# Splitting the last superblock of a graph network's edge loop and moving the work around it

## The chip, the core and the metric

The kernel runs on one core of a Trainium2 chip. The core has five engines that run on their own and meet at semaphores: TensorE (PE in the profile, with PEld for its weight loads), VectorE (DVE), ScalarE (ACT), GpSimd (POOL) and SyncE (SP). Data moves through 16 DMA engines that all queues share. The metric is the device time of one execution in microseconds; the median of the runs counts.

## The reference

A graph of 6250 nodes and 100,000 edges goes through two layers of typed attention and a final layer norm. Node types are 0 to 15, edge types 0 to 31; there are 8 heads of 16. Cut to what matters:

```python
def gt_layer(x, ntype, etype, src, dst, Wk, Wq, Wv, Wa, Watt, Wmsg, pri, skip, g, b):
    k, q, v = (typed_linear(x, ntype, W).reshape(n, H, HS) for W in (Wk, Wq, Wv))
    kT = jnp.einsum('nhd,htdo->nhto', k, Watt)      # one row per node and edge type
    vT = jnp.einsum('nhd,htdo->nhto', v, Wmsg)
    kw = kT[src, :, etype]
    m = vT[src, :, etype]
    a = jnp.einsum('ehd,ehd->eh', kw, q[dst]) * pri[:, etype].T / SQRT_D
    att = edge_softmax(a, dst, n)
    hag = jax.ops.segment_sum((m * att[:, :, None]).reshape(-1, H * HS), dst, num_segments=n)
    h = jax.nn.silu(typed_linear(hag, ntype, Wa))
    alpha = jax.nn.sigmoid(skip[ntype])[:, None]
    h = h * alpha + x * (1.0 - alpha)
    mu = jnp.mean(h, axis=-1, keepdims=True)
    var = jnp.mean((h - mu) ** 2, axis=-1, keepdims=True)
    return (h - mu) * jax.lax.rsqrt(var + 1e-05) * g + b

for l in range(2):
    h = gt_layer(h, ...)
x = _layernorm(x + h @ ff_w + ff_b)
```

## The kernel before

**Tables.** Each layer has a table in DRAM with one row of 256 numbers (`kT` and `vT`, 1 KiB) for every node and edge type. The first layer's table is written during preparation, from the input `x`. The second layer's is written while the first layer runs, from its results. No gather of layer 1 may start before every row of its table is written; a dependency from all the table scatters to the first gather of layer 1 sees to that (lines 969 to 976).

**Nodes in blocks.** Preparation sorts the nodes by class of type and by degree and puts them into 50 blocks of 128. Block `b` has `KB[b]` slots, as many as the largest number of edges into one of its nodes; all blocks together have 867. Class `c` of types (four types each) owns ten blocks with 25, 22, 20, 19, 18, 17, 16, 16, 15 and 14 slots; the other ten blocks hold nodes of mixed types. Blocks are worked on in superblocks of up to four, listed in `sbs` (lines 783 to 792), 15 of them. The last four are: superblock 11, blocks 46 to 49 (mixed, 38 slots); 12, blocks 30 to 33 (86 slots); 13, blocks 34 to 36 (18, 17 and 16 slots); 14, blocks 37 to 39 (16, 15 and 14 slots).

**The edge loop** (`edges`, line 833, once for each layer). For each slot of a block GpSimd issues one indirect DMA that fetches 128 table rows (128 KiB) into `kv` (line 966). Four slots make a chunk; there are 12 chunk buffers. VectorE multiplies a chunk by the queries (line 978) and adds up over each head (line 982). `finished` (line 875) then makes a block's softmax and weighted sums, as a generator whose steps are taken between the chunks of the next block. The last block of a superblock hands its sums to `nodes`.

**Nodes** (line 1056) is a long chain for a whole superblock: normalizing (`hag`, line 1014), transposes, the typed linear `wa` with one mask for each type, tanh, mixing with the old row (`hs`, line 1083), the layer norm with some twelve tiny VectorE instructions, transposes again. In layer 0 the linears for the next layer's keys, values and queries follow (line 1136), and then `pieces_of` (line 1177) makes table rows: for a block, two halves of 16 edge types each, built in `st` (16 KiB in each partition) by 16 small matmuls and PSUM copies on ScalarE (lines 262 to 269), and sent off by GpSimd as an indirect scatter of 2 MiB (line 1183). A block has two such scatters, and `st` has three buffers. The last superblock (`final`, line 1059) shares the copies between ScalarE and VectorE. In layer 1 a linear `ffw`, the addition of `x` and a second layer norm follow, and each block's result goes out by one indirect scatter on GpSimd (line 1216). If the superblock is not `final`, the result is first held in `results` and leaves after a number of further chunks (`leave`, line 862).

**The order.** The program is straight-line code. GpSimd executes in the order in which the program text issues, gathers and scatters in one queue; on the other engines a scheduler at compile time may move an instruction that it holds to be ready ahead of others. The order itself is made by `tick` (line 846): after each of the three parts of a chunk it takes steps of the first generator in `work` (queries and nodes) and of the first in `pieces` (table rows). How many depends on the rate given to `spread`: so many steps over so many gathers. For `nodes` the rate is 34, 46 or 50 steps over `pace(s + 1)`, the slots of the next superblock without half of its first block. For table rows it is 8 steps for each block and 4 more over the slots of superblock `s + 2`, or over 0.6 of them for the last four superblocks. What is left in both lists when the gathers end is issued then (lines 996 to 1003).

**Buffers that count here.** The pool `npl` of the node chain gives most of its tiles one buffer (`hs`, `th`, `mv`, `bn`, `v`), four to the masks `xm`; the node chain has two PSUM buffers (`nb`), the table rows three (`tb`).

Of the kernel before, what the change touches and what calls it, by code (L numbers as in the profile page):

```python
# [27 lines left out]
NC = 4  # L28
# [68 lines left out]
def kernel(  # L97
# [31 lines left out]
    TC = TY // NC  # L129
# [90 lines left out]
    def superblocks(n):  # L220
        k = -(-n // SB)
        for c in range(k):
            yield n * c // k, n * (c + 1) // k - n * c // k
# [216 lines left out]
    with tc.tile_pool(name="tp", bufs=2) as tp, \  # L440
# [302 lines left out]
        sbs = list(superblocks(NT))  # L743
# [26 lines left out]
    def arm(fast):  # L770
# [3 lines left out]
        outs_put, results = [], []  # L774
# [8 lines left out]
        sbs = []  # L783
        if fast:

            mixed = [(NC * CB + i0, k, range(TY)) for i0, k in superblocks(1 + RB)]
            for c in range(NC):
                for i0, k in reversed(list(superblocks(CB))):
                    sbs.append((c * CB + CB - i0 - k, k, range(c * TC, (c + 1) * TC)))
                sbs += mixed[c * len(mixed) // (NC - 1):(c + 1) * len(mixed) // (NC - 1)]  # L790
        else:
            sbs = [(i0, k, range(TY)) for i0, k in superblocks(NB)]
# [40 lines left out]
        def edges(l):  # L833
# [4 lines left out]
            got, work, pieces = [], [], []  # L838
# [3 lines left out]
            def spread(work, gen, steps, slots):  # L842

                work.append([gen, steps / slots, 0.0])
# [12 lines left out]
            def rush(of, gen):  # L857
                while any(w[0] is gen for w in of):
                    for _ in of.pop(0)[0]:
                        pass  # L860
# [8 lines left out]
            def slots(s):  # L869
                return sum(KB[b] for b in range(sbs[s][0], sbs[s][0] + sbs[s][1]))  # L870
# [4 lines left out]
            def finished(s, i, chunks, kvt, a, sums, den):  # L875


                i0, k, _ = sbs[s]
                K = KB[i0 + i]
                av = a[:, :K, :]  # L880
                nc.vector.tensor_tensor(
                    av, av, neg[:, KO[i0 + i]:KO[i0 + i] + K].unsqueeze(2)
                    .to_broadcast([P, K, H]), op=ALU.add)
                yield
                m = ep.tile([P, H], F32, name="m")
                nc.vector.tensor_reduce(m, av.rearrange("p k h -> p h k"), axis=AX.X, op=ALU.max)
                yield
                nc.vector.tensor_tensor(av, av, m.unsqueeze(1).to_broadcast([P, K, H]),  # L888
                                        op=ALU.subtract)
                nc.scalar.activation(av, av, AF.Exp)  # L890
                yield
                yield
                nc.vector.tensor_reduce(den[:, i, :], av.rearrange("p k h -> p h k"),
                                        axis=AX.X, op=ALU.add)

                acc = ep.tile([P, CH, D], F32, name="acc", bufs=1)
                for j in range(len(chunks) + 1):
                    if j < len(chunks):
                        j0, j1 = chunks[j]
                        v = kvt[j][:, :j1 - j0, D:]  # L900
                        nc.vector.tensor_tensor(  # L901
                            (v if j else acc).rearrange("p k (h d) -> p k h d", h=H),
                            v.rearrange("p k (h d) -> p k h d", h=H),
                            av[:, j0:j1, :].unsqueeze(3).to_broadcast([P, j1 - j0, H, HS]),
                            op=ALU.mult)
                    if j > 1:
                        j0, j1 = chunks[j - 1]
                        nc.vector.tensor_tensor(acc[:, :j1 - j0], kvt[j - 1][:, :j1 - j0, D:],  # L908
                                                acc[:, :j1 - j0], op=ALU.add)
                    yield  # L910
                nc.vector.tensor_reduce(sums[:, i, :], acc.rearrange("p k c -> p c k"),
                                        axis=AX.X, op=ALU.add)
                if i == k - 1:
                    spread(work, nodes(l, *sbs[s], sums, den, got[s][1], lambda gen: table(s, gen)),
                           50 if l else 34 + (12 if len(sbs[s][2]) > TC else 0), pace(s + 1))

            def pace(s):
                s = min(s, len(sbs) - 1)
                return slots(s) - 0.5 * KB[sbs[s][0]]
# [3 lines left out]
            def table(s, gen):  # L923


                if gen is None:
                    if s - 2 in tables:
                        rush(pieces, tables[s - 2])
                else:
                    tables[s] = gen  # L930
                    spread(pieces, gen, 8 * sbs[s][1] + 4, (1.0 if s + 4 < len(sbs) else 0.6) * slots(min(s + 2, len(sbs) - 1)))

            before = iter(())
            q = query(0, 0)
            for s, (i0, k, types) in enumerate(sbs):
# [6 lines left out]
                for i in range(k):  # L942
# [17 lines left out]
                    for j0, j1 in chunks:  # L960
                        c = j1 - j0
# [30 lines left out]
                    if not then:  # L992
                        step(end=True)
                    before = finished(s, i, chunks, kvt, a, sums, den)
                    q = then[0] if then else None
            for _ in before:
# [3 lines left out]
            while work or pieces:  # L1000
                for of in (work, pieces, pieces, pieces):
                    if of and next(of[0][0], of) is of:
                        of.pop(0)

        def normalized(acc, den, i0, k):
            rd = ep.tile([P, SB, H], F32, name="rd")
            nc.vector.reciprocal(rd[:, :k], den[:, :k])
            yield
            nc.vector.tensor_tensor(
                rd[:, :k], rd[:, :k],  # L1010
                nonempty[:, i0:i0 + k].unsqueeze(2).to_broadcast([P, k, H]), op=ALU.mult)
            yield
            hag = ep.tile([P, SB, D], F32, name="hag", bufs=1)
            nc.vector.tensor_tensor(  # L1014
                hag[:, :k].rearrange("p i (h d) -> p (i h) d", h=H),
                acc[:, :k].rearrange("p i (h d) -> p (i h) d", h=H),
                rd[:, :k].rearrange("p i h -> p (i h)").unsqueeze(2).to_broadcast([P, k * H, HS]),
                op=ALU.mult)
            return hag
# [194 lines left out]
        def put_out(o, i0, i):  # L1214
            b = i0 + i
            put = nc.gpsimd.indirect_dma_start(  # L1216
                out=out, out_offset=bass.IndirectOffsetOnAxis(ap=node[:, b:b + 1], axis=0),
                in_=o[:, i, :], in_offset=None, bounds_check=N - 1, oob_is_err=False)

            if fast:  # L1220
                for other in outs_put:
                    tc.declare_no_dep(put.ins, other.ins, reason="rows of other nodes")
                outs_put.append(put)
# [69 lines left out]
        for l in range(L):  # L1293
            if l == 0:
                for i, w in enumerate((Wk, Wv, Wq)):
                    load_typed(wkqv[:, i], w[1])
                load_edge_weights(1)
                if not fast:
                    scale_edge_weights()
            else:  # L1300
                load_typed(wa, Wa[1])
            if fast:
                edges(l)
            else:
                edges_any(l)

    full = nc.values_load(over[0:1, 0:1], min_val=0, max_val=1)
    with tc.If(full < 1) as cmp:  # L1308
        with ExitStack() as ctx2:
            ctx2.enter_context(tc.manual_schedule(engines={mybir.EngineType.Pool}))  # L1310
            arm(True)
    with cmp.Else():
        with ExitStack() as ctx2:
            arm(False)
# [46 lines left out]
```

## Time and profile before

| | us |
|---|---|
| median of 3 runs (lowest, highest) | 3544.61 (3541.61, 3552.11) |
| the profiled execution | 3932.2 |
| its span, first to last instruction | 3930.4 |
| first gather of layer 0 starts | 843.5 |
| last gather of layer 0 starts | 2405.5 |
| first gather of layer 1 starts | 2497.5 |
| last gather of layer 1 starts | 3879.9 |
| last output scatter starts | 3922.3 |

The profiled execution is 388 us longer than the median, so its times are compared among themselves. Over the whole span the engines are busy for these shares, and in 40 equal slices for these tenths (PEclk is the clock granted to TensorE, the last two rows are the DMA engines):

```profile
PE 1974.2 (50%) x7142; PEld 887.1 (23%) x7142; DVE 2232.3 (57%) x4900; ACT 833.8 (21%) x1366; POOL 2104.1 (54%) x2032
## 2 busy tenths in 40 slices
PE   4999998950556367655766867202111122021212
PEld 2444553320222123222222323001010111010111
DVE  4787684424736456555745744346446465564746
ACT  1444434430123113421343144100000000000000
POOL 0000005637566566667556763476576676766764
PEclk9999999965667677677767777655555555555555
DMA  5676648793265346755566578533232233323321
GB/s 137 274 305 278 267 194 323 308 319 96 86 240 203 130 154 218 286 200 199 196 247 213 170 280 312 196 100 89 83 95 88 83 98 92 104 85 88 101 85 49
```

A slice is 98 us. Slices 0 to 8 are the preparation, 9 to 24 layer 0, and from 25 on layer 1, where ScalarE and TensorE have little to do. No engine is busy throughout: 54% of POOL is an average over a preparation without gathers and two loops with them.

### The profile page before, as it was taken

What the parts mean: (1) busy time and instruction counts of PE and PEld (TensorE: products, weight loads), DVE (VectorE), ACT (ScalarE), POOL (GpSimd) and SP (SyncE); (2) the same over time, 40 slices, a digit from 0 to 9 for tenths busy, and PEclk for the clock granted to TensorE, in tenths of its full rate; (3) what the DMA queues carried; (4) which work ended last, traced back from release to release, by engine and by line L of the source; (5) the groups of instructions that cost most, each with busy time, mean ns of one, the idle gap of its engine ahead of it and who ended that gap; (6) DMA issues with size and microseconds to landing.
All of it is one profiled execution on the core that took longest, in us unless ns stands there. A gap on an engine that the chain in (4) does not pass through costs nothing. (4 is left out here: it accounts for less than half of the span.)

```text
span 3930.4 us, 25592 instructions
## 1 busy us (share of the span) xinstructions
PE 1974.2 (50%) x7142; PEld 887.1 (23%) x7142; DVE 2232.3 (57%) x4900; ACT 833.8 (21%) x1366; POOL 2104.1 (54%) x2032
## 2 busy tenths in 40 slices
PE   4999998950556367655766867202111122021212
PEld 2444553320222123222222323001010111010111
DVE  4787684424736456555745744346446465564746
ACT  1444434430123113421343144100000000000000
POOL 0000005637566566667556763476576676766764
PEclk9999999965667677677767777655555555555555
DMA  5676648793265346755566578533232233323321
GB/s 137 274 305 278 267 194 323 308 319 96 86 240 203 130 154 218 286 200 199 196 247 213 170 280 312 196 100 89 83 95 88 83 98 92 104 85 88 101 85 49
DMA packets 201147, 694.54 MB, mean 177 GB/s; under 512 B 61382, under 2 KB 111896, under 8 KB 175946
## 3 DMA queue, kind: packets, MB, share of 16 engines
q0 software_dynamic: 105424, 448.83, 34.2%
q1 hardware_dynamic: 72924, 234.11, 15.3%
q10 hardware_dynamic: 22642, 9.82, 1.1%
q8 instruction: 60, 0.98, 0.1%
q14 instruction: 97, 0.79, 0.1%
HBM read 268.12 MB, written 429.48 MB: 177 GB/s over the span
## 5 line engine op out<-in xcount | busy, mean ns | idle before, releaser
L966 POOL DMA_INDIRECT kv<-tab,ell x1734 | 1806.1, 1042 | 786.2 <-issue 501.0
L269 ACT COPY st<-tb 128x512 f32<-128x512 f32 (+1 forms) x976 | 683.1, 764 | 743.1 <-PE tb L262 458.4
L978 DVE TENSOR_TENSOR kv<-kv,q 128x512 f32<-128x512 f32 (+3 forms) x468 | 301.7, 647 | 469.2 <-DMA kv<-tab,ell 426.2
L732 PE MATMUL l<-xm,wkqv 128*128 128x512 f32 (+1 forms) x832 | 385.8, 599 | 54.8 <-DVE xm L232 54.8
L247 PE MATMUL nb<-ident,hag 128*128 128x128 f32 x100 | 25.4, 390 | 763.0 <-DVE hag L1014 350.1
L232 DVE SCALAR_TENSOR_TENSOR xm<-ntb,nb 128x384 f32<-128x384 bf16 (+1 forms) x336 | 186.7, 593 | 245.2 <-remote 158.4
L982 DVE TENSOR_REDUCE a<-kv 128x32 f32<-128x512 f32 (+3 forms) x468 | 297.2, 639 | 29.4 <-remote 6.5
L262 PE MATMUL tb<-bdv,kvT 32*128 32x512 f32 x800 | 276.5, 817 | 43.5 <-ACT st L269 24.8
L241 PE MATMUL nb<-xm,wa 128*128 128x384 f32 (+1 forms) x384 | 219.1, 731 | 151.2 <-DVE xm L232 91.0
L262 PE MATMUL tb<-bdk,kvT 32*128 32x512 f32 x800 | 256.4, 814 | 57.8 <-ACT st L269 35.5
L890 ACT ACTIVATE a<-a 128x128 f32<-128x128 f32 (+12 forms) x100 | 31.9, 319 | 1143.3 <-DVE a L888 487.1
L1183 POOL DMA_INDIRECT tab<-st,row x100 | 110.2, 1102 | 306.7 <-ACT st L269 265.7
L908 DVE TENSOR_TENSOR acc<-kv,acc 128x512 f32<-128x512 f32 (+3 forms) x368 | 233.2, 634 | 57.7 <-remote 47.6
L901 DVE TENSOR_TENSOR kv<-kv,a 128x512 f32<-128x512 f32 (+3 forms) x368 | 231.0, 636 | 0.0
L267 DVE COPY st<-tb 128x512 f32<-128x512 f32 (+1 forms) x208 | 149.2, 718 | 121.9 <-PE tb L262 88.4
L732 PEld LDWEIGHTS l<-xm,wkqv 128*128 128x128 f32 x832 | 149.0, 193 | 286.7 <-issue 199.1
L232 DVE SCALAR_TENSOR_TENSOR xm<-ntb,hT 128x512 f32<-128x512 int32 (+1 forms) x208 | 133.8, 658 | 139.7 <-PE l L732 102.1
L247 PE MATMUL nb<-ident,hs 128*128 128x128 f32 x100 | 32.1, 456 | 353.8 <-DVE hs L1094 274.9
L241 PE MATMUL nb<-xm,wq 128*128 128x384 f32 (+1 forms) x192 | 104.3, 704 | 179.4 <-DVE xm L232 159.1
L247 PEld LDWEIGHTS nb<-ident,hag 128*128 128x128 f32 x100 | 15.2, 193 | 781.7 <-issue 568.2
L720 POOL DMA_DIRECT2D ntb<-in_node_type_dram x13 | 7.3, 558 | 341.9 <-DVE xm L232 341.9
L262 PE MATMUL tb<-bdv,yT 32*128 32x512 f32 x784 | 169.7, 658 | 4.7 <-ACT st L269 3.5
(234 smaller groups left out, 2678.0 us busy)
## 6 DMA issues: line engine op xcount, KB each, us to landing
tab<-st SPq DMA_DIRECT2D x98, 2048.0 KB
kv<-tab,ell POOLq DMA_INDIRECT x1734
hr<-xrd SPq DMA_DIRECT2D x20, 192.0 KB
xrd<-xr POOLq DMA_DIRECT2D x11, 256.0 KB
hr<-in_x_dram POOLq DMA_DIRECT2D x10, 256.0 KB
ntb<-in_node_type_dram POOLq DMA_DIRECT2D x10, 256.0 KB
hr<-xrd SPq DMA_DIRECT2D x10, 256.0 KB
ntb<-typed SPq DMA_DIRECT2D x20, 96.0 KB
```

The costliest lines, as they stand in the source:

```text
L232: nc.vector.scalar_tensor_tensor(xm[:, :n], ntb[:, :n], float(t), hT[:, :n], op0=ALU.is_equal, op1=ALU.mult)
L241: nc.tensor.matmul(ps[:, :n], w[:, t, :], xm[:, :n], start=(t == types[0]), stop=(t == types[-1]))
L262: nc.tensor.matmul(pt[:, b], yT[s, i * P:(i + 1) * P], bd[s, tt, :], start=True, stop=True)
L267: nc.vector.tensor_copy(to, pt)
L269: nc.scalar.copy(to, pt)
L732: nc.tensor.matmul(ps[i][:, :n], wkqv[:, i, t, :], xm[:, :n], start=(t == 0), stop=(t == TY - 1))
L901: nc.vector.tensor_tensor((v if j else acc).rearrange("p k (h d) -> p k h d", h=H), v.rearrange("p k (h d) -> p k h d", h=H), av[:, j0:j1, ...
L908: nc.vector.tensor_tensor(acc[:, :j1 - j0], kvt[j - 1][:, :j1 - j0, D:], acc[:, :j1 - j0], op=ALU.add)
L966: get = nc.gpsimd.indirect_dma_start(out=kv[:, j - j0, :], out_offset=None, in_=tabs[l][:], in_offset=bass.IndirectOffsetOnAxis(ap=ell[:, ...
L978: nc.vector.tensor_tensor(kk, kk, q.unsqueeze(1).to_broadcast([P, c, D]), op=ALU.mult)
L982: nc.vector.tensor_reduce(a[:, j0:j1, :], kk.rearrange("p k (h d) -> p k h d", h=H), axis=AX.X, op=ALU.add)
L1183: put = nc.gpsimd.indirect_dma_start(out=tabs[1].rearrange("(n t) c -> n (t c)", t=16), out_offset=bass.IndirectOffsetOnAxis(ap=row2[:, tg ...
```

## The change

In the list of superblocks the last one, blocks 37 to 39, is cut into blocks 37 and 38 and block 39 alone; there are 16 superblocks then, and only the last counts as `final`. The order of the blocks and of the gathers stays. Node steps of the last three superblocks are spread over 0.6 of `pace`. Table pieces of the last five (the same superblocks as the last four before, since there is one more) are spread over 0.4 of the slots in place of 0.6. For superblocks 12 and 13 these slots are fewer, too, since superblock `s + 2` is now smaller: 31 slots in place of 45 for 12, 14 in place of 45 for 13. After the loop that empties `work` and `pieces`, results that are still held are put out.

```diff
@@ -787,6 +787,10 @@
             for c in range(NC):
                 for i0, k in reversed(list(superblocks(CB))):
                     sbs.append((c * CB + CB - i0 - k, k, range(c * TC, (c + 1) * TC)))
+                if c == NC - 1:
+
+                    i0, k, types = sbs.pop()
+                    sbs += [(i0, k - 1, types), (i0 + k - 1, 1, types)]
                 sbs += mixed[c * len(mixed) // (NC - 1):(c + 1) * len(mixed) // (NC - 1)]
@@ -912,7 +916,8 @@
                     spread(work, nodes(l, *sbs[s], sums, den, got[s][1], lambda gen: table(s, gen)),
-                           50 if l else 34 + (12 if len(sbs[s][2]) > TC else 0), pace(s + 1))
+                           50 if l else 34 + (12 if len(sbs[s][2]) > TC else 0),
+                           (0.6 if s + 3 >= len(sbs) else 1.0) * pace(s + 1))
@@ -928,7 +933,7 @@
                     tables[s] = gen
-                    spread(pieces, gen, 8 * sbs[s][1] + 4, (1.0 if s + 4 < len(sbs) else 0.6) * slots(min(s + 2, len(sbs) - 1)))
+                    spread(pieces, gen, 8 * sbs[s][1] + 4, (1.0 if s + 5 < len(sbs) else 0.4) * slots(min(s + 2, len(sbs) - 1)))
@@ -1001,6 +1006,8 @@
                 for of in (work, pieces, pieces, pieces):
                     if of and next(of[0][0], of) is of:
                         of.pop(0)
+            while results:
+                put_out(*results.pop(0)[1])
```

## The prediction

> **What bounds the kernel now.** I read the busy times by stage first, then GpSimd's (POOL's) instructions in order of time at the two places where the gathers end, then VectorE (DVE), ScalarE (ACT) and TensorE (PE) there. The chain that ended last is of no use: it holds only the last output scatters. By stage (us, busy time and count of each engine, granted clock, DMA share, GB/s):
>
> ```profile
> 1205.00:2406.00 1201.00, 769.00 (x2230) 315.29 (x2227) 698.32 (x1547) 355.87 (x466) 762.79 (x728) 0.73 0.60 213
> 2406.00:2497.00 91.00, 65.83 (x237) 26.24 (x237) 32.93 (x68) 38.93 (x49) 12.50 (x13) 0.74 0.75 303
> 2497.00:3881.00 1384.00, 242.63 (x607) 138.41 (x607) 778.71 (x1988) 44.77 (x123) 950.64 (x911) 0.53 0.32 92
> 3881.00:3931.00 50.00, 13.88 (x35) 8.22 (x35) 24.58 (x95) 1.26 (x3) 8.45 (x6) 0.53 0.04 12
> ```
>
> Layer 1 (third row) is a stream of POOL issues: 911 of them, 950.6 us busy, and 0.30 us of sequencing ahead of most, so 1224 of 1384 us. The change adds none there. What it can move is the second row (91 us between the layers, 12 table scatters, no gather) and the fourth (50 us after the last gather). POOL in order of time at the first (start us, us, engine, line, operation):
>
> ```profile
> 2384.53 1.01 POOL L1183 DMA_INDIRECT tab<-st,row  x1 [0.30 <-issue]
> 2390.87 1.01 POOL L1183 DMA_INDIRECT tab<-st,row  x1 [0.30 <-issue]
> ...
> 2405.54 0.95 POOL L966 DMA_INDIRECT kv<-tab,ell  x1 [0.31 <-issue]
> 2416.52 1.01 POOL L1183 DMA_INDIRECT tab<-st,row  x1 [10.03 <-ACT st L269]
> ...
> 2464.65 0.97 POOL L1183 DMA_INDIRECT tab<-st,row  x1 [15.49 <-ACT st L269]
> 2467.25 0.97 POOL L1183 DMA_INDIRECT tab<-st,row  x1 [1.62 <-DVE st L267]
> 2470.57 0.97 POOL L1183 DMA_INDIRECT tab<-st,row  x1 [2.35 <-DVE st L267]
> 2475.98 0.97 POOL L1183 DMA_INDIRECT tab<-st,row  x1 [4.43 <-DVE st L267]
> 2481.14 0.98 POOL L1183 DMA_INDIRECT tab<-st,row  x1 [4.19 <-DVE st L267]
> 2486.91 0.97 POOL L1183 DMA_INDIRECT tab<-st,row  x1 [4.79 <-issue]
> 2497.51 0.99 POOL L966 DMA_INDIRECT kv<-tab,ell  x1 [9.63 <-issue]
> ```
>
> The reader is to see three things: a scatter per four gathers (every 6.3 us) while gathers last; 92.0 us from the last gather of layer 0 to the first of layer 1; and scatters some 5 us apart once pieces are plentiful. That 5 us is the transfer: one scatter is 2 MiB, and between 2470 and 2490 us the DMA share is 1.0 at 419 to 429 GB/s, so 4.9 us each. The stretch from 2286 to 2497 us moves 28 scatters (59 MB) and 66 gathers (8.7 MB), 158 us at that rate; about 50 us of DMA idleness is all that reordering could win between the layers.
>
> VectorE and POOL at the end of the kernel:
>
> ```profile
> 3893.60 0.56 DVE L1014 TENSOR_TENSOR hag<-sums,rd 128x384 f32<-128x384 f32 x1
> ...
> 3919.68 0.98 POOL L1216 DMA_INDIRECT out_dram<-o,node  x1 [25.50 <-DVE o L1169]
> 3920.97 0.98 POOL L1216 DMA_INDIRECT out_dram<-o,node  x1 [0.30 <-POOLq L1308]
> 3922.26 0.98 POOL L1216 DMA_INDIRECT out_dram<-o,node  x1 [0.30 <-issue]
> ```
>
> The last gather starts at 3879.9; 13.7 us later the last sums are normalized, and 26.1 us after that the last superblock's results leave.
>
> **What the Trainium skill says.** "DMA: Bandwidth & Descriptors", Specifications, gives a fabric ceiling of 435 GB/s; the 429 GB/s of the final scatters agrees. Its section on the anatomy of a SWDGE DMA adds about 2 us of fixed cost to each; in a row of scatters the trace shows 5.0 to 5.8 us, so the fixed part overlaps, and I use the trace. "PSUM — Partial Sum Buffer", Engine vs sequencer instructions, calls the ScalarE, VectorE and GpSimd queues strict FIFO; the trace agrees: at 2416.52 POOL stood 10.03 us for one piece, with nothing behind it overtaking. This is what the slower rival rests on.
>
> **The change part by part.** I number superblocks 0 to 15 as after; 13 is the same in both, 14 was blocks 37 to 39 (16, 15 and 14 slots) and becomes 37 and 38, with 39 alone as 15. Walking the pace rule of the loop through both programs gives where scatters stand among the 867 gathers; the walk of the old program lies on the trace scatter for scatter. Before: superblock 11's eight between gathers 805 and 830, 12's eight between 834 and 857, 13's and 14's six each after gather 867. After: 11's between 801 and 818, 12's between 826 and 834, 13's six between 850 and 853, and only 14's four and 15's two after 867. The node steps of 13 still begin at 838 but end at 850, not 867.
>
> Loop of layer 0. Sixteen scatters now stand ahead of gather 835, too dense to hide: 16 x 5.0 us plus 33 gathers x 0.3 us (128 KiB at 429 GB/s) = 90 us. From 2284 (the first scatter was issued at 2286.2 after a stand of 8.0 us; being four gathers earlier helps it little) this is 2374, where gather 834 was at 2343.0. Sixteen gathers free of scatters at 1.25 us: 2394 (before 2378.2). Then 13's six scatters, two intervals at ACT's copying rate (four copies of 0.93 us) and three at 5.0, some 24 us with what lies between: 2418. Fourteen gathers at 1.25 us: the last at 2436. It was 2405.5, so **+30 us**.
>
> Between the layers. Before, 92.0 us. After: finishing block 39 took 19.0 us to 2424.5, of which 9.0 were a stand for ACT, busy with 13's copies, that are gone now: 10. The chain of the last superblock, from `hag` at 2424.5 to its first scatter at 2464.65, took 40.1; 7.7 of these were a stand of VectorE for PE behind 13's matmuls, also gone; one block instead of three shortens matmuls (9.5 us for the three linears, 4.2 for the first), masks (1.95) and evacuations, and I take 10 of the some 20 us that scale: 22.4. Superblock 14's chain runs beside it and they share single buffers (`hs`, `th`), two PSUM buffers and four masks: 0 to 10, I take 6. A second scatter 3, and its landing and the wait of the first gather 10.6 as before. Sum 52, so **-40 us**. Superblock 14 itself is not late: its sums are there when the last gathers are issued, a two-block chain is some 26 us, and four scatters follow by then plus 15. Between the layers with the loop: -10.
>
> Layer 1 and the end. Gathers, scatters and output scatters keep their counts, so the POOL stream stays. Node steps of 13 end at gather 846 instead of 865, which frees VectorE at the end of some 4 us (its statistics and normalizing lay between 3879.9 and 3888.3). Superblock 14's chain can start at block 38's sums, 3885.3 in the trace, two or three us sooner so freed; a two-block chain is 26.1 less about 6, plus 4 for block 39's finishing beside it: 3906. Block 39's chain cannot overlap all of it: `mv` has one buffer, held until the last use of 14's means at its output step, so 15 runs from its `mv` on after that: 15.1 us in the trace (3904.6 to 3919.7) less six of nine matmuls (4 us) and about 1 of narrower steps: 10. First output scatter 3916, and the two held results of 14 leave behind it at 1.29 us each; the last starts at 3918.7, not 3922.3: **-3.5 us**. That the held results leave once the work is emptied is needed, since 14 is no longer the final one; it costs no issue, as three stand at the end in both. The extra superblock adds one query load of layer 1 and one small query stage of layer 0 (some 4 transposes and matmuls and 3 evacuations), beside gathers, near nothing; if not covered, 3 us.
>
> Sum: -10 - 3.5 = -13 against the profiled execution's 3932.2 us (span 3930.4). The unprofiled median is 388 us lower; I cannot see from this trace where those go, though issues of POOL are many enough. My terms are transfer times and dependency chains, so I carry -13 over whole: 3544.6 - 13 = **3532 us**.
>
> **The rivals.**
> - *Slower: POOL stands for superblock 13's first piece.* Place: its scatters at gather 850, ahead of the last 17 gathers in POOL's queue. The chain of 13 took from `hag` at 2335.0 to 2416.5, 81.5 us, while mixed with 12's pieces on PE and ACT. Gather 822 would be at about 2330, sums 14 us later as before (2319.3 to 2333.4), so the chain starts at 2345. I assume it is done by 2394, since it is spread over 12 gathers instead of 29 and a free chain is 40.1 - 7.7 = 32 us. If it takes 81.5 again, POOL stands 33 us: -13 + 33 = +20, 3565. Up to 13 us the gain stays; from 24 us on it is slower by more than 0.3%. For it: PE and ACT issue 12's pieces ahead. Against: more of these are done by then.
> - *Full gain.* Denser pieces of 11 start at 2276, where their first copy was (8 us sooner), and the two last chains don't hinder each other (6): -27, 3518. For it: DMA has the room. Against: the stands on ACT that the trace shows already.
> - *Nothing: what leaves the boundary is paid in the loop.* Gathers share DMA with dense scatters, and each lands behind up to three of them (15 us); if 11 of these are exposed at block 38 or 39, the sum is -2: 3543. For it: loop and boundary differ by +30 and -40, each of that size by estimate.
>
> **How the numbers follow.** Forecast 0.45, full gain 0.15, nothing 0.15, slower 0.25. A measurement tells about 0.3% from no change, 10.6 us. Of the forecast 0.40 is beyond that, so faster 0.55, same 0.20, slower 0.25. The forecast's own range is 3522 to 3540. The whole range goes down past the full gain with sums ready earlier, 3512, and up to most of the slower rival, 3560.
>
> **What would show it.** In the profile after: 22 scatters before layer 0's last gather and six after; that gather some 30 us later than 2405.5; the gap to layer 1 near 52 us; POOL's idle time before 13's first scatter under 13 us; layer 1's gather stream at 1384 us; and the last output scatter 38 to 40 us after the last gather. A long stand of POOL at gather 850, a gap still over 75 us, or a layer 1 that moves by over 10 us would make the prediction wrong.

## The result and the profile after

| | before | after |
|---|---|---|
| median, us (runs; lowest to highest) | 3541.61 (7; 3533.27 to 3554.62) | 3576.00 (7; 3567.71 to 3595.64) |
| ratio after to before, 95% interval | 1 | 1.0091 [1.0065, 1.0118] |

The change makes the kernel slower by 0.9%, some 32 us. The forecast was 3532 us, faster; 3576 lies above its range.

One thing has to be known before two profiles are laid side by side. Chips differ. On one of them the same kernel takes 3920 us without a profiler, too (first experiment), and its profile there agrees with the one that the prediction reads (spans 3900.5 and 3930.4, layer 1 1384.2 and 1382.4 us); I take that one to come from such a chip. The profile of after (span 3573.4) came from one at the speed of the medians. So after is compared here with a later profile of before at that speed (span 3555.3, a run of 3557.1 us, experiment `e9_before_third`). I number gathers of layer 0 from 1 to 867 and cut the time at gathers 801, 835, 850, 854, 867, the first gather of layer 1 and its last gather. Busy time by stretch, first before, then after (start and end, length, busy time and count on PE, PEld, DVE, ACT and POOL, granted clock, DMA share, GB/s):

```profile
2087.00:2153.00 66.00, 49.39 (x183) 19.63 (x183) 35.05 (x78) 38.38 (x45) 44.64 (x44) 0.77 0.81 295
2153.00:2182.00 29.00, 21.61 (x73) 8.75 (x71) 18.92 (x53) 14.81 (x19) 20.01 (x20) 0.65 0.99 375
2182.00:2191.00 9.00, 6.88 (x20) 2.51 (x20) 1.17 (x2) 6.70 (x7) 5.75 (x7) 0.61 1.01 404
2191.00:2210.00 19.00, 17.15 (x48) 8.02 (x46) 11.49 (x23) 4.96 (x9) 13.50 (x14) 0.73 0.95 372
2210.00:2295.00 85.00, 61.91 (x222) 24.20 (x220) 33.61 (x69) 36.19 (x46) 13.26 (x15) 0.75 0.80 323
2295.00:3506.00 1211.00, 232.09 (x607) 137.79 (x607) 770.24 (x1986) 44.98 (x123) 922.43 (x911) 0.54 0.36 105
```
```profile
2070.00:2162.00 92.00, 74.75 (x269) 29.66 (x265) 35.38 (x81) 57.24 (x65) 51.08 (x50) 0.74 0.89 344
2162.00:2183.00 21.00, 11.08 (x21) 5.64 (x22) 13.53 (x45) 1.18 (x3) 14.33 (x15) 0.58 0.83 300
2183.00:2226.00 43.00, 32.23 (x118) 11.58 (x116) 12.86 (x25) 24.78 (x30) 10.02 (x11) 0.82 0.69 273
2226.00:2244.00 18.00, 5.12 (x12) 3.10 (x12) 10.68 (x35) 0.79 (x2) 13.74 (x15) 0.50 0.63 219
2244.00:2308.00 64.00, 38.29 (x160) 20.04 (x160) 20.57 (x59) 22.99 (x35) 7.06 (x8) 0.74 0.60 233
2308.00:3522.00 1214.00, 234.08 (x607) 138.34 (x607) 770.86 (x1989) 44.50 (x122) 925.35 (x911) 0.53 0.36 104
```

Read three columns. Length: the first stretch grew from 66 to 92 us, the third (four gathers) from 9 to 43; the gap between the layers shrank from 85 to 64; layer 1 stayed. ACT's busy time: before, copies for table rows run through all of the loop's end (14.8, 6.7 and 5.0 us in the second to fourth row); after, ACT has 1.2 us of work in 21 and 0.8 in 18, and 24.8 between them. DMA share: 0.99, 1.01 and 0.95 before while the last 32 gathers were issued, 0.83, 0.69 and 0.63 after. The old order kept the DMA engines full with evenly spread scatters. The new one sends them in bursts; between these ACT has next to nothing to do, PE is busy for a half and a quarter of the time, and DMA is not filled.

At the place where 13's scatters stand now, POOL after, in order of time:

```profile
2183.39 0.95 POOL L971 DMA_INDIRECT kv<-tab,ell  x1 [0.30 <-issue]
2196.52 1.02 POOL L1190 DMA_INDIRECT tab<-st,row  x1 [12.18 <-ACT st L269]
...
2207.71 0.97 POOL L1190 DMA_INDIRECT tab<-st,row  x1 [2.88 <-ACT st L269]
...
2224.91 1.30 POOL L1190 DMA_INDIRECT tab<-st,row  x1 [11.06 <-ACT st L269]
2226.51 1.35 POOL L971 DMA_INDIRECT kv<-tab,ell  x1 [0.30 <-issue]
...
2243.80 0.94 POOL L971 DMA_INDIRECT kv<-tab,ell  x1 [0.30 <-issue]
2268.40 1.01 POOL L1190 DMA_INDIRECT tab<-st,row  x1 [23.65 <-ACT st L269]
...
2294.71 0.97 POOL L1190 DMA_INDIRECT tab<-st,row  x1 [13.59 <-ACT st L269]
2297.23 0.97 POOL L1190 DMA_INDIRECT tab<-st,row  x1 [1.54 <-issue]
2307.60 0.99 POOL L971 DMA_INDIRECT kv<-tab,ell  x1 [9.40 <-DMA tab<-st,row]
```

Twice POOL stands for a table piece while 17 and 14 gathers are queued behind it: 12.18 us for 13's first, 11.06 us for its sixth. After the last gather it stands 23.65 us for 14's first piece and 13.59 us for 15's. Why 13's first piece is so late is seen earlier, on PE, ACT and VectorE (in this order):

```profile
2155.89 3.70 PE L262 MATMUL tb<-bdv,kvT 32*128 32x512 f32 x8
2159.52 0.90 PE L247 MATMUL nb<-ident,hag 128*128 128x128 f32 x3
```
```profile
2145.33 3.76 ACT L269 COPY st<-tb 128x1024 f32<-128x1024 f32 x4 [2.30 <-DMA tab<-st,row]
2151.61 2.84 ACT L269 COPY st<-tb 128x1024 f32<-128x1024 f32 x3 [2.52 <-DMA tab<-st,row]
```
```profile
2134.98 0.56 DVE L1021 TENSOR_TENSOR hag<-sums,rd 128x384 f32<-128x384 f32 x1
...
2146.75 0.69 DVE L983 TENSOR_TENSOR kv<-kv,q 128x512 f32<-128x512 f32 x1 [11.21 <-DMA kv<-tab,ell]
...
2163.13 0.69 DVE L983 TENSOR_TENSOR kv<-kv,q 128x512 f32<-128x512 f32 x1 [14.97 <-DMA kv<-tab,ell]
...
2164.47 1.94 DVE L232 SCALAR_TENSOR_TENSOR xm<-ntb,nb 128x384 f32<-128x384 bf16 x4
```

`hag` of superblock 13 is ready at 2135.5, but PE transposes it only at 2159.52, 24.0 us later: until then PE makes 12's table rows, which stand ahead of it. These move at the speed of ACT's copies, and ACT waits in turn for scatters that still hold the buffers `st` (2.30 and 2.52 us); the DMA share in these 24 us is 1.02, at 403 GB/s. VectorE's two long waits for gathers (11.21 and 14.97 us) lie mostly within that time. The masks need the transposes, and come another 4 us after these, at 2164.47, since on VectorE they stand behind the product of a chunk whose gathers, issued among 12's scatters, it awaits until 2163.13. From the masks to the first scatter it is 32.0 us (2164.47 to 2196.52), during which ACT stood 9.91 and 10.48 us, for PE. Before, where 12's pieces are spread over more gathers, the same transposes come 7.0 us after `hag` (VectorE, then PE):

```profile
2142.54 0.56 DVE L1014 TENSOR_TENSOR hag<-sums,rd 128x384 f32<-128x384 f32 x1
```
```profile
2150.09 0.55 PE L247 MATMUL nb<-ident,hag 128*128 128x128 f32 x3
```

The sixth piece waits on ACT (the last line is VectorE's):

```profile
2213.96 2.84 ACT L269 COPY st<-tb 128x1024 f32<-128x1024 f32 x3 [1.40 <-DMA tab<-st,row]
2223.43 0.30 ACT L894 ACTIVATE a<-a 128x120 f32<-128x120 f32 x1 [6.63 <-DVE a L892]
2223.64 0.99 ACT L269 COPY st<-tb 128x1024 f32<-128x1024 f32 x1
```
```profile
2221.22 0.56 DVE L983 TENSOR_TENSOR kv<-kv,q 128x384 f32<-128x384 f32 x1 [28.47 <-DMA kv<-tab,ell]
```

Its fourth copy stands behind block 38's exponential (`a`, L894), which waits for VectorE, and VectorE had stood 28.47 us for the gathers that complete block 38. These (851 to 853, at 2208.99 to 2211.56) had been issued right behind four scatters of 2 MiB, and VectorE's wait for them ended 9.7 us after the last was issued. So a scatter waits for a copy, the copy for a softmax, the softmax for gathers, and these for the scatters before them.

### The profile page after: what moved, and what is told of

It is laid out like the page before. It is cut to its first block, busy times and chain, and to the rows that moved or that the text cites. A ratio compares the mean times of both kernels' runs of the same rounds, so it can differ in the third digit from the quotient of the medians.

```text
span 3573.4 us, 25772 instructions
## 1 busy us (share of the span) xinstructions
PE 1932.1 (54%) x7190; PEld 888.7 (25%) x7190; DVE 2221.2 (62%) x4955; ACT 839.8 (24%) x1383; POOL 2057.8 (58%) x2032
## 5 line engine op out<-in xcount | busy, mean ns | idle before, releaser
L971 POOL DMA_INDIRECT kv<-tab,ell x1734 | 1769.4, 1020 | 614.9 <-issue 471.0
L894 ACT ACTIVATE a<-a 128x128 f32<-128x128 f32 (+12 forms) x100 | 31.9, 319 | 1237.4 <-DVE a L892 1197.1
L262 PE MATMUL tb<-bdv,kvT 32*128 32x512 f32 x800 | 267.3, 791 | 64.6 <-ACT st L269 64.2
L241 PE MATMUL nb<-xm,wa 128*128 128x384 f32 (+3 forms) x400 | 214.7, 703 | 110.8 <-DVE xm L232 110.7
L262 PE MATMUL tb<-bdk,kvT 32*128 32x512 f32 x800 | 245.9, 799 | 13.9 <-ACT st L269 13.9
L232 DVE SCALAR_TENSOR_TENSOR xm<-ntb,nb 128x384 f32<-128x384 bf16 (+3 forms) x352 | 187.7, 573 | 79.5 <-PE nb L247 44.6
L267 DVE COPY st<-tb 128x512 f32<-128x512 f32 (+1 forms) x200 | 139.7, 699 | 104.6 <-PE tb L262 87.5
L241 PE MATMUL nb<-xm,wq 128*128 128x384 f32 (+3 forms) x200 | 100.7, 663 | 134.2 <-DVE xm L232 131.1
```

Of the source, the lines that this page charges most:

```text
L232: nc.vector.scalar_tensor_tensor(xm[:, :n], ntb[:, :n], float(t), hT[:, :n], op0=ALU.is_equal, op1=ALU.mult)
L241: nc.tensor.matmul(ps[:, :n], w[:, t, :], xm[:, :n], start=(t == types[0]), stop=(t == types[-1]))
L262: nc.tensor.matmul(pt[:, b], yT[s, i * P:(i + 1) * P], bd[s, tt, :], start=True, stop=True)
L267: nc.vector.tensor_copy(to, pt)
L971: get = nc.gpsimd.indirect_dma_start(out=kv[:, j - j0, :], out_offset=None, in_=tabs[l][:], in_offset=bass.IndirectOffsetOnAxis(ap=ell[:, ...
```

## The experiments

Each kernel was timed beside before on its chip; the first four ran on the chip at 3920 us, the others on two chips at 3555 and 3551 us. Two readings were to be told apart at first: that the rates (table pieces and node steps over fewer gathers) make the loss and the split gains, or that the split with its extra superblock makes it. The table below gives for every profile of these runs how long the stretches are, cut as above: gathers 801 to 854 and 854 to 867 of layer 0, the gap to layer 1, the sum of these, layer 1 from first to last gather, and from there to the last output scatter (us).

| run | ratio to before | 801-854 | 854-867 | gap | sum | layer 1 | end |
|---|---|---|---|---|---|---|---|
| before, `e9_before_third` | 0.9998 | 103.3 | 19.6 | 84.4 | 207.3 | 1211.0 | 41.4 |
| after | 1.0091 | 156.6 | 17.3 | 63.8 | 237.6 | 1214.3 | 43.2 |
| `e10_split_only` | 1.0000 | 107.3 | 19.8 | 76.2 | 203.3 | 1208.7 | 43.6 |
| `e11_rates_only` | 1.0138 | 154.3 | 16.6 | 75.2 | 246.1 | 1211.9 | 40.4 |
| `e12_nodes_only` | 1.0036 | 114.6 | 21.2 | 80.8 | 216.6 | 1210.6 | 41.1 |
| `e7_held_13` | 1.0021 | 118.0 | 19.8 | 74.1 | 211.8 | 1210.5 | 43.5 |
| `e8_held_13_tail` | 1.0018 | 118.9 | 19.8 | 75.9 | 214.6 | 1212.7 | 40.7 |
| `e6_only_13` | 1.0054 | 118.9 | 39.2 | 65.6 | 223.7 | 1215.2 | 43.4 |
| `e5_dense_11_12` | 1.0037 | 117.3 | 16.7 | 85.6 | 219.7 | 1208.6 | 43.4 |
| chip at 3920: `e1_before_again` | 1.0004 | 111.9 | 19.0 | 93.6 | 224.5 | 1384.2 | 41.6 |
| `e2_split_only` | 0.9987 | 116.0 | 21.9 | 78.4 | 216.3 | 1382.0 | 47.9 |
| `e3_rates_only` | 1.0099 | 160.3 | 16.7 | 75.3 | 252.3 | 1383.6 | 39.9 |
| `e4_after_old_pieces` | 0.9990 | 125.9 | 21.3 | 73.2 | 220.4 | 1388.6 | 45.6 |

What comes before gather 801 is the same work in all of them, and its time scatters by itself: from the first gather to gather 801 it took 1221 to 1237 us in the nine profiles from the other chips, in no order with the kernels. So single spans are not compared, but stretches, and medians for the verdict. A stretch scatters less: `e7_held_13` and `e8_held_13_tail`, with the same rates in layer 0, differ by 2.8 us in the sum.

**Before once more.** No edit. It asks whether the 388 us between the first profile and the median are the profiler's.

> The kernel before, unchanged, for a second profile. Theory A (the first profile was disturbed, since its layer loops ran at 1.8 and 1.6 us a gather against 1.6 and 1.4 in the profile of the changed kernel, although most of both programs is the same): span near 3540, loops at about 1.6 and 1.4 us a gather, and the stretch from gather 750 to the first gather of layer 1 near 285 us, against 320 in the changed kernel. Theory B (the profile of before is true to the program): span again near 3930.

Measured: 3917.72 us beside 3919.97 us of before, unprofiled, on one chip; ratio 1.0004 [0.9978, 1.0029]; span 3900.5. They are not the profiler's: that chip takes 3920 us.

**The split alone**, with the old rates for pieces and node steps:

```diff
-                           (0.6 if s + 3 >= len(sbs) else 1.0) * pace(s + 1))
+                           (37.0 if s == 13 else pace(s + 1)))
...
-                    spread(pieces, gen, 8 * sbs[s][1] + 4, (1.0 if s + 5 < len(sbs) else 0.4) * slots(min(s + 2, len(sbs) - 1)))
+                    spread(pieces, gen, 8 * sbs[s][1] + 4,
+                           {11: 30.6, 12: 27.0, 13: 27.0}.get(s) or (1.0 if s < 11 else 0.6) * slots(min(s + 2, len(sbs) - 1)))
```

> Only the last superblock is split (and held results drained); the scatters of superblocks 11, 12 and 13 and the node steps of 13 keep the rates of before. Theory A (the scatters put ahead of the last gathers cost the time: POOL stands for pieces with gathers behind): no slower than before, 3525 to 3545. Theory B (the split costs it: a second chain of nodes at the end that waits for single buffers in both layers): slower by 15 us or more, 3555 or above.

Measured: ratio 0.9987 [0.9965, 1.0009], no difference that can be told. The gap is 15 us shorter than in the first experiment, the loop 7 and the end 6 us longer. The split isn't the loss.

**The rates alone**, in the program before with its 15 superblocks:

```diff
-                           50 if l else 34 + (12 if len(sbs[s][2]) > TC else 0), pace(s + 1))
+                           50 if l else 34 + (12 if len(sbs[s][2]) > TC else 0),
+                           13.8 if s == 13 else pace(s + 1))
...
-                    spread(pieces, gen, 8 * sbs[s][1] + 4, (1.0 if s + 4 < len(sbs) else 0.6) * slots(min(s + 2, len(sbs) - 1)))
+                    spread(pieces, gen, 8 * sbs[s][1] + 4,
+                           {11: 20.4, 12: 12.4, 13: 5.6}.get(s) or slots(min(s + 2, len(sbs) - 1)))
```

> The last superblock stays whole; scatters of 11, 12 and 13 and the node steps of 13 get the rates of the changed kernel, so that 22 scatters stand before the last gather of layer 0 as there. Theory A: slower than before by 25 to 45 us, 3565 to 3590. Theory B: within 10 us of before.

Measured: ratio 1.0099 [1.0059, 1.0138]. The sum of the stretches grows by 27.8 us (224.5 to 252.3), and the loss is 0.99% of 3920, 39 us. The rates are the loss.

**After with the old rate of pieces** (split and new node rates stay):

```diff
-                    spread(pieces, gen, 8 * sbs[s][1] + 4, (1.0 if s + 5 < len(sbs) else 0.4) * slots(min(s + 2, len(sbs) - 1)))
+                    spread(pieces, gen, 8 * sbs[s][1] + 4,
+                           {11: 30.6, 12: 27.0, 13: 27.0}.get(s) or (1.0 if s < 11 else 0.6) * slots(min(s + 2, len(sbs) - 1)))
```

> The changed kernel with the table pieces of superblocks 11, 12 and 13 at the rates of before; the faster node steps and the split stay. Theory A: the loss goes, 3525 to 3550. Theory B: it stays, 3565 to 3590. If the faster node steps of 13 are what hurts (VectorE stands for them in the loop), this is slow and the split alone is not.

Measured: ratio 0.9990 [0.9963, 1.0017]. With the old rate of pieces no loss can be told on this chip, though gathers 850 to 854 still take 20.3 us in place of 7.8: the node rate costs something of its own there.

**Which pieces.** Three kernels part the rate of pieces; each is after but for the same line. With the dense pieces of 11 and 12, and 13's held back until the gathers have ended:

```diff
+                           {11: 20.4, 12: 12.4, 13: 1.0e6}.get(s) or (1.0 if s < 11 else 0.6) * slots(min(s + 2, len(sbs) - 1)))
```

> The changed kernel, but the table pieces of superblock 13 are made after the last gather; those of 11 and 12 stay as dense as in the change. On a chip where before runs at about 3920. Theory A1 (the six scatters of 13 ahead of the last 14 gathers are the loss): near before or a little faster, 3900 to 3925, and 131 to 145 us from gather 801 to 867. Theory A2 (the density of 11 and 12 is the loss): still slow, 3945 or above, and over 160 us there.

Measured: 1.0037 [1.0021, 1.0052]. Gathers 801 to 854 take 14.0 us more than before, and the gap, with 12 scatters again, is 85.6. Neither theory had this: part of the loss is here, and part isn't.

With 13's pieces ahead of the last gathers as in after, and the old rates for 11 and 12:

```diff
+                           {11: 30.6, 12: 27.0, 13: 5.6}.get(s) or (1.0 if s < 11 else 0.6) * slots(min(s + 2, len(sbs) - 1)))
```

> The changed kernel, but 11 and 12 have the rates of before; the six scatters of 13 still go ahead of the last gathers (at gathers 861 to 865). Theory A1: still slow, 3940 to 3960, a stand of POOL of 20 us or more ahead of 13's scatters. Theory A2: near before, 3910 to 3925.

Measured: 1.0054 [1.0036, 1.0073]. Gathers 854 to 867 take 39.2 us in place of 19.6, as 13's scatters come right behind 12's there; the gap pays back 18.8. The stand of 20 us that I expected ahead of 13's first scatter isn't there (0.30 us); POOL stands 4.78 and 5.77 us for the third and fourth, while ACT waits 2.29 and 2.52 us for scatters that hold its buffers.

With neither:

```diff
+                           {11: 30.6, 12: 27.0, 13: 1.0e6}.get(s) or (1.0 if s < 11 else 0.6) * slots(min(s + 2, len(sbs) - 1)))
```

> The changed kernel with the rates of before for 11 and 12 and all pieces of 13 after the last gather; its node steps of 13 stay fast. Both theories: the loop is that of before (131 us from gather 801 to 867), the gap to layer 1 is 70 to 75 us in place of 93.6, so 3895 to 3912, faster than before by some 15 us if the end of layer 1 stays within 4 us.

Measured: 1.0021 [1.0011, 1.0032], where I had expected a gain of some 15 us: gathers 850 to 854 take 22.7 us in place of 9.1, since POOL stands 15.38 us there for a piece of 12. Taken in one order, the steps from before to after are, by the sums of the table: the split -4.0 us, the new node rates (and 13's pieces after the gathers) +8.6, 13's pieces ahead of the last gathers +11.9, the dense pieces of 11 and 12 +13.9; together +30.4. By the ratios, times 3550 us: 0.0, +7.5, +11.7, +13.1, together +32. The two accounts agree within 4 us in each step. In another order the parts share differently: dense pieces cost 7.8 us while 13's are held back.

**The end of layer 1.** Held 13 as above, held results put out inside the loop that empties the lists, and second buffers for the layer norm's small tiles, `mv` among them:

```diff
-            while results:
-                put_out(*results.pop(0)[1])
+                while results:
+                    put_out(*results.pop(0)[1])
...
-            mv = npl.tile([P, SB, 2], F32, name="mv")
+            mv = npl.tile([P, SB, 2], F32, name="mv", bufs=2)
...
```

> As e7_held_13, with two buffers for the small tiles of the layer norm (mv, bn, v, gi, ri, t), and the held results of superblock 14 leave as soon as they are made and not behind those of 15. Theory M (15's chain waits at the end for mv): the last output scatter 35 to 38 us after the last gather instead of 43 to 48. Theory N (it waits for something else, as one of the two PSUM buffers of the node chain): only the 2.6 us of the two scatters are won, 41 to 45 us.

Measured: 1.0018 [1.0008, 1.0028]; the end took 40.7 in place of 43.5 us, with the output scatters of 14 at 3530.93 and 3532.22 and the last at 3541.33, where without the edit all three came from 3543.62 on. These 2.8 us are about the two issues of 1.29 us that no longer stand ahead of 15's. So the single `mv` that I had put on the path was not on it, and the difference to the kernel without this edit (1.0021) can't be told in the medians.

**Before, the split and the rates again**, on a chip at 3551 us, since the first such runs were on the other chip; the edits are those above.

> The kernel before once more, for a profile on a chip where it runs at about 3550. Both theories of its profile: span near 3550. Where does the changed kernel lose 32 us to it? Theory A (in the stretch from gather 801 to the first gather of layer 1, 237.7 us in the changed kernel): 203 to 210 us there, both layer loops and the end as in the changed kernel. Theory C (also elsewhere, as the order of instructions moved in the loops): the stretch is 224 us as in the slower profile, and the rest lies in the loops.

> The split alone again, on this chip. It was 0.9987 of before where before runs at 3920. If e7's loss of 0.2% against before comes from the split: 1.001 to 1.003 here; if it comes from the node steps of 13: 0.997 to 1.000.

> The rates alone again, on this chip. It was 1.0099 of before where before runs at 3920. Theory A: 1.009 to 1.013 here, the whole loss of the change or more. If the split shares in the loss here: 1.004 to 1.008.

Measured: before against itself 0.9998 [0.9986, 1.0010]; the split alone 1.0000 [0.9984, 1.0016]; the rates alone 1.0138 [1.0112, 1.0164], more than after itself. So with the new rates the split helps, by 8.5 us of stretches: with three blocks in the last superblock POOL stood 41.40 us after the last gather, where after it stood 23.65 and 13.59.

**The node rate alone**, in the program before:

```diff
-                           50 if l else 34 + (12 if len(sbs[s][2]) > TC else 0), pace(s + 1))
+                           50 if l else 34 + (12 if len(sbs[s][2]) > TC else 0),
+                           13.8 if s == 13 else pace(s + 1))
```

> The kernel before with only the node steps of superblock 13 spread over 13.8 gathers in place of 37, in both layers; pieces and superblocks as before. If node steps are free: 0.997 to 1.001. If VectorE stands for them in the loops: 1.002 or above, the loop from gather 801 to 867 longer by 6 us or more.

Measured: 1.0036 [1.0021, 1.0051], some 13 us for a change of which I had reckoned only gains. In its profile POOL stands for a piece of superblock 12 (first line), and PE shows what stood in its way (the other):

```profile
2186.30 1.02 POOL L1184 DMA_INDIRECT tab<-st,row  x1 [13.30 <-ACT st L269]
```
```profile
2170.69 6.96 PE L1137 MATMUL nb<-xm,wkqv 128*128 128x384 f32 x16 [4.99 <-DVE xm L232]
```

The linears of 13's nodes, issued earlier now, stand on PE ahead of 12's pieces: PE waited 4.99 us for their masks, then spent 6.96 us on 16 matmuls, and a scatter with gathers queued behind it waited 13.30 us.

No version beat before. The best is the split alone, the same within 0.16% on the chip at 3551.

## Why the prediction was wrong

It had the sign of each stretch up to the first gather of layer 1 right, and the sum wrong: -10 us for layer 0's end and the gap, where +30.4 was measured. Its steps, with differences against before at the same speed:

| step | predicted, us | measured, us |
|---|---|---|
| gathers 801 to 835, dense scatters of 11 and 12 | +28.5 | +26.7 |
| gathers 835 to 850, free of scatters | -12.6 | -7.5 |
| gathers 850 to 854, 13's six scatters | +16.3 | +34.0 |
| gathers 854 to 867 | -2.2 | -2.3 |
| gap between the layers | -40 | -20.6 |
| layer 1's stream | 0 | +3.3 |
| after the last gather | -3.5 | +1.8 |

**The step that failed first is 13's chain.** The prediction had it start at 2345 and assumed "it is done by 2394, since it is spread over 12 gathers instead of 29 and a free chain is 40.1 - 7.7 = 32 us". It took 61.5 us from `hag` to its first scatter (2134.98 to 2196.52), in place of 49, because it had to let 12's pieces by first. `hag` came in time (48.4 us before gather 850), but PE transposed it 24.0 us after it was ready, behind the matmuls of 12's table rows, and the masks stood 4 us more behind a chunk on VectorE; from the masks on it took 32.0 us, about what was reckoned for a free chain. The four kernels with dense pieces of 11 and 12 agree on the step that failed: from `hag` to its transposes it is 24.0 us in after, 24.1 in `e11_rates_only`, 23.5 in `e5_dense_11_12` and 25.8 in `e3_rates_only`, against 5 to 7 us where 11 and 12 keep their old rates and the last superblock is whole, and 16 to 18 where it is split. The prediction's own figures could have said it: its row of dense scatters ends at 2374, a free chain behind it ends at 2406, and gather 850 is at 2394. That makes a stand of 12 us; the trace has 12.18, a match that is closer than such figures can promise.

"PSUM — Partial Sum Buffer", Engine vs sequencer instructions, which calls the queues of ScalarE, VectorE and GpSimd strict FIFO, was applied in the prediction to POOL alone. VectorE and ACT show the same in this trace: the masks behind a chunk that waits until 2163.13, the copy behind the exponential at 2223.64; and so does PE with the transposes of `hag`. So POOL stood 12.18 us for the first piece, where I had taken nothing, and 11.06 for the sixth; the six took 43.1 us from gather 850 to 854 in place of 24.

**The slower rival was right in its place and mechanism, and wrong in its point of decision.** It had POOL stand for 13's first piece at gather 850, because PE and ACT take 12's pieces ahead of 13's chain, and that is what the traces show. I gave it 0.25, on the ground that more of these pieces would be done by then. It kept the gain for a stand of "up to 13 us". The stand was 12.18, inside that, and the kernel is slower all the same, for the sixth piece's stand, a gap that gave half of what was forecast, and node steps that cost. The rival "nothing" had the delay of the gathers, that land "behind up to three of them (15 us)", and VectorE's 14.97 is of that size; but it counted it once, at block 38 or 39, and not where it holds up 13's chain and the sixth piece. I had the two halves in two rivals and put them together in none.

**The gap.** -40 was mis-sized in two terms. From the last gather to the last sums it was 19.0 us in the first profile, of which 9.0 was a stand that I expected gone; at the speed of the medians it is 10.3 before (2210.36 to 2220.62), so there was nothing to gain, and after it is 12.0. The chain of the last block, taken as 22.4 and 6, measured 38.9 (2255.82 to 2294.71), hardly less than the 41.3 for three blocks before (2220.62 to 2261.90):

```profile
2255.82 0.29 DVE L1021 TENSOR_TENSOR hag<-sums,rd 128x128 f32<-128x128 f32 x1
2272.35 0.88 DVE L232 SCALAR_TENSOR_TENSOR xm<-ntb,nb 128x128 f32<-128x128 bf16 x4 [16.24 <-PE nb L247]
```

16.24 us of it VectorE waited for the transpose of `hag`, which PE ran at 2271.98, behind 14's linears (from 2253.59) and the first matmuls of 14's table rows, which move at the speed of ACT's copies. Splitting a superblock doesn't overlap its halves when an in-order engine has the first one's table rows ahead of the second one's first step. The six scatters fewer after the last gather did bring what they could: from 15's first scatter to layer 1's first gather it is 12.9 us, where before it was 32.9 from 14's first.

**Node steps over fewer gathers** were costed only as gains. Alone they lose 0.36%, some 13 us, the size of the stand of 13.30 us shown above. In layer 1 "node steps of 13 end at gather 846 instead of 865" did not hold as a time: after, the last gather is at 3521.86, and 13's results (`o`) leave VectorE 6.3 us later, at 3528.11 (before: 7.0 us later), since its tiny steps are taken between those of the chunks. So the two or three us for 14 did not come.

**The end.** The last step is as reckoned: from `mv` of 15 to its output step it took 9.1 us (3552.72 to 3561.77), predicted 10. But `mv` came 30.9 us after the last gather, where the prediction had it after 14's output step, 26 us after it (3906 less 3879.9). 15's chain was late for the reason seen in layer 0: PE ran the transpose of 15's `hag` at 3546.65, last in a row with the matmuls of 14's `ffw`. On PE, then on VectorE:

```profile
3541.54 0.74 PE L247 MATMUL nb<-ident,hs 128*128 128x128 f32 x2 [6.80 <-DVE hs L1101]
...
3546.07 0.80 PE L1169 MATMUL nb<-xr,ident 128*128 128x128 f32 x2
3546.65 0.42 PE L247 MATMUL nb<-ident,hag 128*128 128x128 f32 x1
```
```profile
3539.95 0.29 DVE L1021 TENSOR_TENSOR hag<-sums,rd 128x128 f32<-128x128 f32 x1
...
3547.39 0.26 DVE L232 SCALAR_TENSOR_TENSOR xm<-ntb,nb 128x128 f32<-128x128 bf16 x1
...
3552.72 0.18 DVE L1060 BATCH_NORM_AGGREGATE mv<-bn 128x2 f32<-128x6 f32 x1
```

`hag` of 15 stood ready 6.4 us on PE (3540.24 to 3546.65), which had idled 6.80 us for 14's `hs` only just before, and the masks came at 3547.39. The second buffers of the eighth experiment left this untouched.

**What held.** 22 scatters ahead of layer 0's last gather and six after it, as walked; layer 1's stream unchanged; "DMA: Bandwidth & Descriptors", Specifications, with its 435 GB/s as the ceiling of the dense row: 404 GB/s in the stretch before where the DMA share is 1.01. And the bound worked out there, "about 50 us of DMA idleness is all that reordering could win", was right as a bound (62 gathers, not 66, stand in its stretch, which is 1 us); the new order made more idleness, not less.

**What is open.** By how much the order on PE alone (15's transpose behind 14's pieces) would shorten the gap was not tried. That 13's chain is late by PE's order, and the sixth piece by gathers that land late, is read from the traces; thinning out 11 and 12 shortens the first, but no run moved 13's transposes ahead of 12's matmuls, or ACT's copies ahead of the exponential, by themselves.

## What to carry to other kernels

Work issued into an in-order queue earlier is not done earlier if its producer isn't: look for what the producer's own queue has ahead of it, and whether that waits for the very transfers you are making denser. Where the DMA share is already close to 1, as the 0.95 to 1.01 here, packing transfers has little to gain and can open holes elsewhere. Cost "fewer gathers for the same steps" as a reordering of each engine's queue, not as time saved, and take durations for stretches from a profile whose own time matches the median.

## What was not expected of the hardware

Two chips ran the same program at 3920 and 3550 us, at almost the same mean granted clock (0.70 and 0.715) and with the same minimal issue on POOL (0.94 us and 0.30 between). The difference lies all over both gather loops: 1384.2 against 1211.0 us in layer 1, and 1388.3 against 1234.3 from the first gather of layer 0 to gather 801. Waits of VectorE in most of layer 1, before on the chip at 3920 (line, what for: us in total, times, longest us), then the same on one at 3551:

```profile
DVE kv L978 <- DMA kv<-tab,ell: 189.2, 73, 5.7
DVE xm L232 <- remote: 35.4, 10, 4.9
DVE a L888 <- remote: 21.2, 4, 6.7
```
```profile
DVE kv L978 <- DMA kv<-tab,ell: 361.7, 147, 5.7
```

On the slower chip VectorE stands, for several us at a time, where the profile has no releaser for it ("remote"), even ahead of a step such as `a` (L888) whose inputs are its own results, and it waits less for gathers. On the other chip there are no such stands. VectorE's busy time agrees (778.2 and 770.2 us of layer 1). What holds VectorE up there isn't shown by any run.
